# Attention and two quantised convolutions on one core: q's first stacks from two products, three projections later, v's bias in the output projection

## The chip, the cores and the metric

The kernel runs on one core of a Trainium2 chip. The metric is device time in microseconds (us), the median of several executions. A core has five engines with a queue each, worked off in order: TensorE (PE in the profile, with its weight loads as PEld), VectorE (DVE), ScalarE (ACT), GpSimd (POOL) and SyncE (SP). SP, ACT and POOL also issue DMA transfers. Matmuls write to PSUM, a memory of eight banks; a bank holds 512 float32 numbers for each of the 128 partitions.

## What is computed

Input x has four images of 128 channels and 64 x 64 pixels. The first layer is a group norm (8 groups) with self-attention over the 4096 pixels, four heads of 32 channels, and a residual; the second layer is two 3 x 3 convolutions with 3-bit weights, each followed by a batch norm and relu, the second with a residual. The change touches only the first layer:

```python
x_norm = _group_norm(x, norm_w, norm_b)
qkv = jnp.einsum('oc,bchw->bohw', qkv_w, x_norm) + qkv_b[None, :, None, None]
q, k, v = jnp.split(qkv, 3, axis=1)
...
attn = jnp.einsum('bhid,bhjd->bhij', q, k) * scale
attn = jax.nn.softmax(attn, axis=-1)
out = jnp.einsum('bhij,bhjd->bhid', attn, v)
out = out.transpose(0, 1, 3, 2).reshape(b, c, h, w)
out = jnp.einsum('oc,bchw->bohw', proj_w, out) + proj_b[None, :, None, None]
return x + out
```

Since the rows of a softmax sum to one, a constant added to every row of v comes out of the attention unchanged.

## The kernel before

**Norm.** The group norm is folded into the projection weights. `norm_parts` (line 242) returns nine small steps for an image: `zero` to `four` make from the statistics the scaled weights `wn` (128 x 384, the columns of q, k and v) and a column `c`; `five` and `six` multiply `c` with the weights of k and q and make from it and `qkv_b` the two bias columns `b2`; `five_v` and `six_v` make `bvn`, the bias of v spread over 128 partitions. For image 0 the steps run at the start; for the others they are put into an earlier image's blocks.

**Projections.** An image is cut into 8 chunks of 512 pixels. `project_parts` (line 319) gives for a chunk three products (k, q, v), each in three steps: two halves of matmuls (`mm` or `mmv`, four bands of 32 columns each), then the evacuation of the PSUM bank. For k and q (`parts`) ScalarE writes the rounded high part with the bias added, and VectorE the rest, the low part. For v (`evac_v`) VectorE adds `bvn`. High and low parts of k and q go to DRAM (`kd`, `qd`), and are read back stacked by heads: in a tile of k or q two heads lie with their high and low parts in four bands of 32 partitions (`load_k`, four DMAs on SP; `load_q`, eight). Only for chunk 0 of image 0 are they copied straight between tiles, by eight DMAs each (`direct`).

**PSUM.** The pool `pss` has three places of two banks, tag "s", for the scores; at the start the products of k and q use them too. The pool `psa` has two banks, tag "a": one is held by the accumulator `acc` of the running block, the other is used in turn by everything else (products, the small norm matmuls, row sums `l`, the output projection `po`).

**Blocks.** There are 32 blocks, 8 for each image, a block being 512 queries against the image's 4096 keys in 32 steps `kt` of 128 keys. A step is two pairs of heads: `scores(pair)` makes the scores of two heads with four matmuls of 64 x 128 x 512 and has ScalarE take the exponent. `weights(step, half)` multiplies the exponents with v, a half of the queries at a time. The order of all engines' work is written out by hand: three score pairs, three halves of weights, and so on, with scores three pairs ahead:

```python
    run_scores(3)
    while at["half"] < 2 * steps:
        run_scores(3)
        run_weights(3)
```

The row sums are added up by VectorE (`r`, 128 x 2048 a step), and for six steps of a block by DMAs on POOL's queue that accumulate (`rm`, 1 MB each).

**Side work.** `schedule(n, before)` (line 633) lists for block n what is put after which half: `at_half(p, f)`. `ends` are the last halves of the groups of three. `visit(i, first, second, evacuate, split)` puts a product at group end i (with `split` its second half at the next end), and the evacuation one half later, which in the queues is behind the next group's three scores and exponents. For block 0 the products still missing for image 0 are placed at every second group end: k5, v4, k6, v5, k7, q1, v6, v7 at ends 0, 2, 4, 6, 8, 10, 12, 14; `load_k` of a k chunk is put five halves after its end. k chunk j is read first by pair 8j, and v chunk j by half 8j.

**Start.** Lines 588 to 624: the eight x chunks of image 0 are loaded into two tiles, statistics and norm steps follow (with idle matmuls between them), then ten products: k0, q0, k1, v0, k2, v1, k3, v2, k4, v3, with `five_v` and `six_v` after q0, and `load_k` of the next chunk after each v. DMAs of constants are issued on POOL first (lines 115 to 127).

**Later images.** In the third such block of an image (`qn == 2`), `five` is put at end 1, `six` and `five_v` one half later, `six_v` two halves later. A product of k of the next image stands in the same block at end 3. At a block's end `store` (line 546) adds the projection, its bias `bp` and x.

Of the kernel before, what the change touches and what calls it, by code (L numbers as in the profile page):

```python
# [22 lines left out]
P = 128  # L23
# [55 lines left out]
def _fast_body(ctx, tc, x, norm_w, norm_b, qkv_wt, qkv_b, proj_wt, proj_b,  # L79
# [35 lines left out]
    nw, nb = column(norm_w, "nw"), column(norm_b, "nb")  # L115
    wqkv = const.tile([P, 3 * P], F32, name="wqkv")
    nc.gpsimd.dma_start(out=wqkv, in_=qkv_wt)
    bkq = const.tile([P, 2], F32, name="bkq")
    nc.gpsimd.dma_start(out=bkq[:, 0:1], in_=qkv_b[P : 2 * P].rearrange("(c o) -> c o", o=1))
    nc.gpsimd.dma_start(out=bkq[:, 1:2], in_=qkv_b[0:P].rearrange("(c o) -> c o", o=1))  # L120
    bv = const.tile([P, P], F32, name="bv")
    nc.gpsimd.dma_start(out=bv, in_=qkv_b[2 * P : 3 * P].partition_broadcast(P))
    wp = const.tile([P, P], F32, name="wp")
    nc.gpsimd.dma_start(out=wp, in_=proj_wt)
    bp = column(proj_b, "bp")
# [116 lines left out]
    def norm_parts(b, st):  # L242
        mv = small.tile([P, 2], F32, name=f"mv{b}", tag="mv")
        mean = small.tile([P, 1], F32, name=f"mean{b}", tag="mean")
        dv = small.tile([P, 1], F32, name=f"dv{b}", tag="dv")
        gm = {}

        def zero():
            nc.vector.bn_aggr(mv, st.rearrange("p j s -> p (j s)"))


        def one():
            gm[0] = psa.tile([P, FB], F32, name=f"gm{b}", tag="a")
            nc.tensor.matmul(gm[0][:, 0:1], gavg, mv[:, 0:1], start=True, stop=True)

        def two():
            nc.vector.tensor_tensor(dv, mv[:, 0:1], gm[0][:, 0:1], ALU.subtract)
            nc.vector.scalar_tensor_tensor(dv, dv, dv, mv[:, 1:2], ALU.mult, ALU.add)
            nc.vector.tensor_copy(mean, gm[0][:, 0:1])

        def three():
            gm[1] = psa.tile([P, FB], F32, name=f"gv{b}", tag="a")
            nc.tensor.matmul(gm[1][:, 0:1], gavg, dv, start=True, stop=True)

        def four():
# [12 lines left out]
        def five():  # L278
            wn, c, cb = norm[b]
            gm[2] = psa.tile([P, FB], F32, name=f"gb{b}", tag="a")  # L280
            nc.tensor.matmul(gm[2][:, 0:1], wqkv[:, P : 2 * P], c, start=True, stop=True)
            nc.tensor.matmul(gm[2][:, 1:2], wqkv[:, 0:P], c, start=True, stop=True)

        def six():
            b2 = wpool.tile([P, 2], F32, name=f"b2_{b}", tag="b2")
            nc.vector.tensor_tensor(b2, bkq, gm[2][:, 0:2], ALU.subtract)
# [12 lines left out]
        return zero, one, two, three, four, five, six, five_v, six_v  # L299

# [18 lines left out]
    def project_parts(b, j, xin, start=False):  # L319
# [27 lines left out]
        def parts(what, o, dst):  # L347
# [3 lines left out]
            nc.scalar.activation(hi, ps[what], AF.Identity, bias=bias)  # L351
            nc.vector.scalar_tensor_tensor(lo, ps[what], bias, t[:, 0, :], ALU.add, ALU.subtract)  # L352
            if start and j == 0:
                direct(what, t)
            else:
                (nc.sync if start else nc.gpsimd).dma_start(out=dst[b, j].rearrange("s p n -> p s n"), in_=t)  # L356

# [7 lines left out]
        def evac_v():  # L365
            if b == 0:
                v = vs[b, j] = vpool.tile([P, KB, P], F32, name=f"v{b}_{j}", tag="v")
                v = v.rearrange("p i f -> p (i f)")
            else:
                v = staged(1, "v")[:, 0, :]  # L370
            nc.vector.tensor_tensor(v.rearrange("p (i f) -> p i f", f=P),
                                    ps["v"].rearrange("p (i f) -> p i f", f=P),
                                    norm[b][2].unsqueeze(1).to_broadcast([P, KB, P]), ALU.add)
            if b > 0:
                nc.gpsimd.dma_start(out=vd[b, j], in_=v)

# [11 lines left out]
        qs[b, j] = qpool.tile([P, 2, 2, FB], F32R, name=f"q{b}_{j}", tag="q")  # L388
        return qs[b, j]

    def direct(what, t):

        u = k_tile(0, 0) if what == "k" else q_tile(0, 0)
        engines = (nc.sync, nc.gpsimd) if what == "k" else (nc.scalar, nc.sync, nc.gpsimd)
        for g in range(2):
            for c, s in enumerate((0, 2, 1, 3)):
                i, part = divmod(s, 2)
                h = 2 * g + i
                src = t[h * D : (h + 1) * D, :, :]
                eng = engines[(4 * g + c) % len(engines)]  # L400
                if what == "k":
                    eng.dma_start(out=f32(u)[s * D : (s + 1) * D, g, :], in_=src[:, part, :])
                else:
                    eng.dma_start(out=f32(u)[s * D : (s + 1) * D, g, :, :], in_=src)

    def load_k(b, j):
        k = k_tile(b, j)
# [65 lines left out]
    def finish_parts(n):  # L473
# [124 lines left out]
    zero, one, two, three, four, five, six, five_v, six_v = norm_parts(0, st)  # L598
    zero()
    one()  # L600
    keep_warm(3)
# [23 lines left out]

# [7 lines left out]
    def schedule(n, before):  # L633
# [49 lines left out]
        if b + 1 < B:  # L683
# [727 lines left out]
```

## Time and profile before

| what | us |
|---|---|
| median of three runs (2546.02 to 2547.59) | 2547.48 |
| the profiled execution | 2548.74 |
| its span, first to last instruction | 2547.0 |
| first scores of block 0 | 26.66 |
| convolutions, from the last weights on (2231.4) to the end | 315.6 |

| engine | busy in 34.21 to 105.00 us (70.79 us) |
|---|---|
| PE | 70.79 |
| ACT | 62.41 |
| DVE | 61.23 |
| POOL | 7.89 |

The profiled execution's own time is 1.7 us above its span. In the profile a line such as `L456 PE MATMUL acc<-p,v` names the line of the kernel, the engine, the operation, and the tile written and those read. In a timeline the columns are start and duration in us, then the instruction, how many of the same kind follow each other, and in brackets how long the engine had been idle before, and what ended that. A "q" behind an engine (SPq) means its sequencer, which issues DMAs. The ends of matmuls are modelled, so the starts are the better measure.

### The profile page before, as it was taken

To read this page: it belongs to the slowest core of one execution; us is meant where nothing else is said; L and a number is where in the kernel's file an instruction comes from. 1 tells how busy PE (TensorE), PEld (TensorE's weight loads), DVE (VectorE), ACT (ScalarE), POOL (GpSimd) and SP (SyncE) were. 2 spreads that over 40 slices of the span, in tenths; PEclk is the share of its full clock that TensorE was granted. 3 is DMA by queue.
4 is the path that set the end of the run, shared out by engine and by line. 5 is a ranking of instruction groups with operands and counts; after the bars stand their busy time and mean duration, and the time that the engine had idled before them with its cause. 6 is when DMAs were issued, how large, how long until landed. Compare 5 with 4: busy or idle time off the path is not lost.

```text
span 2547.0 us, 65043 instructions
## 1 busy us (share of the span) xinstructions
PE 2509.0 (99%) x28708; PEld 1503.6 (59%) x28708; DVE 2137.2 (84%) x1402; ACT 2087.4 (82%) x2278; POOL 281.6 (11%) x461
## 2 busy tenths in 40 slices
PE   9999999999999999999999999999999999999995
PEld 6555555555555555555555555555555555577774
DVE  6899888889988889889988888889999999954445
ACT  5999888999988999999988899989999999911224
POOL 2111111111011111110111111111000011000000
PEclk9999999999999999999999999999999999999998
DMA  6877667788757667797766666796666666745004
GB/s 193 192 185 169 168 173 181 171 203 182 184 132 190 170 152 169 164 231 164 173 163 172 157 166 158 191 203 150 149 138 144 146 145 149 150 90 160 1 1 166
DMA packets 148954, 403.86 MB, mean 159 GB/s; under 512 B 59416, under 2 KB 60184, under 8 KB 120120
## 3 DMA queue, kind: packets, MB, share of 16 engines
q0 software_dynamic: 45840, 280.39, 48.2%
q1 hardware_dynamic: 100952, 113.60, 16.9%
q10 hardware_dynamic: 1872, 5.64, 0.6%
q8 instruction: 227, 3.72, 0.6%
q14 instruction: 63, 0.52, 0.1%
HBM read 107.48 MB, written 56.42 MB: 64 GB/s over the span
## 4 chain that ended last, share of the span: by engine, by line
PE 92%; issue 3%; DMA 2%; DVE 1%; ACT 1%; ACTq 0%; POOL 0%; SPq 0%; POOLq 0%; DVEq 0%
PE s L442 41%; PE acc L456 36%; PE c L782 9%; DMA rm<-p 2%; PE l L488 1%; PE pq L317 1%; PE pk L317 1%; PE po L317 1%; PE pv L317 1%; DVE r L471 1%; ACT p L444 0%; ACT res L949 0%; DMA xh<-in_x_dram 0%; PE c_last L782 0%; DVE res L948 0%
## 5 line engine op out<-in xcount | busy, mean ns | idle before, releaser
L444 ACT ACTIVATE p<-s 128x1024 f32<-128x1024 f32 x2048 | 1950.5, 1032 | 201.6 <-PE s L442 154.5
L471 DVE TENSOR_TENSOR r<-r,p 128x2048 f32<-128x2048 f32 x768 | 1758.2, 2289 | 65.0 <-ACT p L444 14.5
L442 PE MATMUL s<-q,k 64*128 64x512 f32 x8192 | 1138.6, 409 | 1.7 <-ACT p L444 0.9
L456 PE MATMUL acc<-p,v 128*32 128x256 f32 x16384 | 1026.4, 383 | 0.0
L442 PEld LDWEIGHTS s<-q,k 64*128 64x128 f32 x8192 | 715.4, 184 | 410.3 <-issue 165.3
L456 PEld LDWEIGHTS acc<-p,v 128*32 128x32 f32 x16384 | 462.4, 109 | 483.7 <-issue 248.5
L466 POOL DMA_DIRECT2D rm<-p x160 | 139.5, 872 | 800.4 <-ACT p L444 535.5
L849 ACT COPY cv<-c 128x512 f32<-128x512 f32 x60 | 35.2, 586 | 200.1 <-DVE st L848 200.1
L782 PE MATMUL c<-hi,wq 128*128 128x512 f32 x540 | 139.1, 401 | 1.3 <-issue 1.3
L782 PE MATMUL c<-lo,wq 128*128 128x512 f32 x540 | 138.5, 400 | 0.0
L848 DVE BATCH_NORM_STATS2 st<-c 128x6 f32<-128x512 f32 x60 | 41.9, 699 | 103.9 <-PE c L782 83.4
L782 PEld LDWEIGHTS c<-hi,wq 128*128 128x128 f32 x540 | 101.2, 188 | 30.3 <-issue 2.1
L782 PEld LDWEIGHTS c<-lo,wq 128*128 128x128 f32 x540 | 101.6, 188 | 27.2
L352 DVE SCALAR_TENSOR_TENSOR kst<-pk,b,kst 128x512 fp32r<-128x512 f32 x32 | 24.0, 751 | 83.6 <-PE s L442 68.5
L469 DVE TENSOR_TENSOR r<-p,p 128x2048 f32<-128x2048 f32 x32 | 73.2, 2288 | 12.1 <-ACT p L444 11.1
L352 DVE SCALAR_TENSOR_TENSOR qst<-pq,b,qst 128x512 fp32r<-128x512 f32 x32 | 24.0, 751 | 58.2 <-PE s L442 47.3
L356 POOL DMA_DIRECT2D qd<-qst x31 | 23.6, 760 | 262.7 <-DVE qst L352 220.8
L492 POOL DMA_DIRECT2D r<-rm x31 | 26.2, 844 | 220.4 <-DMA rm<-p 95.1
L356 POOL DMA_DIRECT2D kd<-kst x27 | 20.0, 740 | 175.8 <-DVE kst L352 167.2
L488 PE MATMUL l<-r,ones 128*32 128x256 f32 (+1 forms) x504 | 37.7, 382 | 0.0
L464 POOL DMA_DIRECT2D rm<-p x32 | 17.8, 557 | 176.8 <-ACT p L444 93.4
L351 ACT ACTIVATE kst<-pk,b 128x512 fp32r<-128x512 f32 x32 | 22.3, 699 | 18.2 <-PE pk L317 18.2
(149 smaller groups left out, 739.3 us busy)
## 6 DMA issues: line engine op xcount, KB each, us to landing
rm<-p POOLq DMA_DIRECT2D x192, 1024.0 KB, 7.9
q<-qd SPq DMA_DIRECT2D x248, 128.0 KB
r<-rm POOLq DMA_DIRECT2D x31, 1024.0 KB, 7.6
x<-in_x_dram SPq DMA_DIRECT2D x86, 256.0 KB
k<-kd SPq DMA_DIRECT2D x124, 128.0 KB
qd<-qst POOLq DMA_DIRECT2D x31, 512.0 KB, 5.3
kd<-kst POOLq DMA_DIRECT2D x27, 512.0 KB, 4.8
y<-x POOLq DMA_DIRECT2D x32, 256.0 KB, 6.2
```

Source lines behind the costliest of these rows:

```text
L317: nc.tensor.matmul(out[cs, :], w[:, cs], x, start=True, stop=True)
L352: nc.vector.scalar_tensor_tensor(lo, ps[what], bias, t[:, 0, :], ALU.add, ALU.subtract)
L356: (nc.sync if start else nc.gpsimd).dma_start(out=dst[b, j].rearrange("s p n -> p s n"), in_=t)
L442: nc.tensor.matmul(s[:, i, :], k[r, half, c0 : c0 + P], q[r, half, part, :], start=(part == 0), stop=(part == 1))
L444: nc.scalar.activation(pts[step][:, 2 * half : 2 * half + 2, :], s, AF.Exp, scale=SCALE)
L456: nc.tensor.matmul(acc[n][h * D : (h + 1) * D, cs], v[:, kt % KB, h * D : (h + 1) * D], pt[:, h, cs], start=(kt == 0 and half == 0), stop= ...
L466: nc.gpsimd.dma_start(out=msum[n], in_=pt, accum_op=ALU.add)
L469: nc.vector.tensor_tensor(rsum[n], pts[step - 1], pt, ALU.add)
L471: nc.vector.tensor_tensor(rsum[n], rsum[n], pt, ALU.add)
L488: nc.tensor.matmul(t["l"][h * D : (h + 1) * D, cs], ones, r[:, h, cs], start=first, stop=end)
L782: nc.tensor.matmul(ps.rearrange("p (r w) -> p r w", w=W), w[:, tap, :], part[:, r0 + kh : r0 + kh + RB, kw : kw + W], start=(n == 0), stop ...
L848: nc.vector.bn_stats(st[:, b * NB + c, :], ps[:, j, :])
```

## The change

It has four parts. (1) The first q tile of image 0 is no longer made from a product that is copied by eight DMAs. `direct_q` makes two products, one for each pair of heads, whose four bands of output partitions already lie as the stack needs them (each head twice); ScalarE writes the high part, VectorE the low part, straight into the tile. It needs the bias of q in the same stacked order, two columns more in `b2` for image 0. (2) Three products (k4, v2, v3) go from the start into block 0, whose side work is spread anew. (3) The bias of v is taken out of v and added by the output projection: `five` makes a third column, `seven_v` multiplies it with the projection's weights, and `eight_v` adds `proj_b`. (4) v's bank is copied by ScalarE, without a bias.

```diff
-    bkq = const.tile([P, 2], F32, name="bkq")
-    nc.gpsimd.dma_start(out=bkq[:, 0:1], in_=qkv_b[P : 2 * P].rearrange("(c o) -> c o", o=1))
-    nc.gpsimd.dma_start(out=bkq[:, 1:2], in_=qkv_b[0:P].rearrange("(c o) -> c o", o=1))
-    bv = const.tile([P, P], F32, name="bv")
-    nc.gpsimd.dma_start(out=bv, in_=qkv_b[2 * P : 3 * P].partition_broadcast(P))
+    bkqv = const.tile([P, 5], F32, name="bkqv")
+    for c, o in enumerate((P, 0, 2 * P)):
+        nc.gpsimd.dma_start(out=bkqv[:, c : c + 1],
+                            in_=qkv_b[o : o + P].rearrange("(c o) -> c o", o=1))
+    for band in range(4):
+        nc.gpsimd.dma_start(
+            out=bkqv[band * D : (band + 1) * D, 3:5],
+            in_=qkv_b[0:P].rearrange("(g i d) -> i d g", i=2, d=D)[band // 2])
...
-            cb = wpool.tile([P, P], F32, name=f"cb{b}", tag="cb")
-            nc.vector.tensor_copy(cb, c.to_broadcast([P, P]))
-            norm[b] = [wn, c, cb]
+            norm[b] = [wn, c, None]
...
-            nc.tensor.matmul(gm[2][:, 0:1], wqkv[:, P : 2 * P], c, start=True, stop=True)
-            nc.tensor.matmul(gm[2][:, 1:2], wqkv[:, 0:P], c, start=True, stop=True)
+            for u, o in enumerate((P, 0, 2 * P)):
+                nc.tensor.matmul(gm[2][:, u : u + 1], wqkv[:, o : o + P], c, start=True, stop=True)
+            if b == 0:
+                for g in range(2):
+                    for band in range(4):
+                        h = 2 * g + band // 2
+                        nc.tensor.matmul(gm[2][band * D : (band + 1) * D, 3 + g : 4 + g],
+                                         wqkv[:, h * D : (h + 1) * D], c, start=True, stop=True)
...
-        def five_v():
-            gm[3] = psa.tile([P, FB], F32, name=f"gw{b}", tag="a")
-            nc.tensor.matmul(gm[3][:, 0:P], norm[b][2], wqkv[:, 2 * P : 3 * P],
-                             start=True, stop=True)
-
-        def six_v():
-            bvn = wpool.tile([P, P], F32, name=f"bvn{b}", tag="bvn")
-            nc.vector.tensor_tensor(bvn, bv, gm[3][:, 0:P], ALU.subtract)
-            norm[b][2] = bvn
+        def seven_v():
+            gm[3] = psa.tile([P, FB], F32, name=f"gp{b}", tag="a")
+            nc.tensor.matmul(gm[3][:, 0:1], wp, norm[b][1][:, 2:3], start=True, stop=True)
+
+        def eight_v():
+            norm[b][2] = small.tile([P, 1], F32, name=f"bpn{b}", tag="bpn")
+            nc.vector.tensor_tensor(norm[b][2], bp, gm[3][:, 0:1], ALU.add)
...
-            nc.vector.tensor_tensor(v.rearrange("p (i f) -> p i f", f=P),
-                                    ps["v"].rearrange("p (i f) -> p i f", f=P),
-                                    norm[b][2].unsqueeze(1).to_broadcast([P, KB, P]), ALU.add)
+            nc.scalar.copy(v, ps["v"])
...
+    def direct_q(xin):
+
+        u = q_tile(0, 0)
         for g in range(2):
...
+            ps = pss.tile([P, 2, FB], F32, name=f"pq_first{g}", tag="s")[:, 0, :]
+            for band in range(4):
+                h = 2 * g + band // 2
+                nc.tensor.matmul(ps[band * D : (band + 1) * D, :], norm[0][0][:, h * D : (h + 1) * D],
+                                 xin, start=True, stop=True)
+            bias = norm[0][1][:, 3 + g : 4 + g]
+            nc.scalar.activation(u[:, g, 0, :], ps, AF.Identity, bias=bias)
+            nc.vector.scalar_tensor_tensor(u[:, g, 1, :], ps, bias, f32(u)[:, g, 0, :],
+                                           ALU.add, ALU.subtract)
...
-            nc.vector.scalar_tensor_tensor(t["x"], t["o"], bp, t["x"], ALU.add, ALU.add)
+            nc.vector.scalar_tensor_tensor(t["x"], t["o"], norm[b][2], t["x"], ALU.add, ALU.add)
...
-    for what, j in (("k", 0), ("q", 0), ("k", 1), ("v", 0), ("k", 2), ("v", 1), ("k", 3), ("v", 2),
-                    ("k", 4), ("v", 3)):
+    for what, j in (("k", 0), ("q", 0), ("k", 1), ("v", 0), ("k", 2), ("v", 1), ("k", 3)):
+        if what == "q":
+            direct_q(halves[0][:, 0, :])
+            continue
         for f in first_chunk(j, what, True):
             f()
-        if what == "q":
-            five_v()
-            six_v()
         if what == "v":
             load_k(0, j + 1)
+    load_k(0, 3)
+    seven_v()
+    eight_v()
...
-            for i, what, j in ((0, "k", 5), (2, "v", 4), (4, "k", 6), (6, "v", 5), (8, "k", 7),
-                               (10, "q", 1), (12, "v", 6), (14, "v", 7)):
+            for i, what, j in ((0, "k", 4), (2, "v", 2), (3, "v", 3), (4, "q", 1), (6, "k", 5),
+                               (8, "v", 4), (9, "v", 5), (10, "k", 6), (12, "v", 6), (13, "k", 7),
+                               (15, "v", 7)):
...
-                at_half(ends[1] + 1, late[b][7])
-                at_half(ends[1] + 2, late[b][8])
+                at_half(ends[3], late[b][7])
+                at_half(ends[3] + 1, late[b][8])
```

The copy of chunk 0 of k by eight DMAs stays, as `direct_k`.

More of the change, by code (lines that the diff above doesn't have):

```diff
@@ L272, in four @@
             nc.vector.tensor_scalar(wn, wqkv, a, None, ALU.mult)
-            cb = wpool.tile([P, P], F32, name=f"cb{b}", tag="cb")
-            nc.vector.tensor_copy(cb, c.to_broadcast([P, P]))
-            norm[b] = [wn, c, cb]
+            norm[b] = [wn, c, None]
         def five():
-            wn, c, cb = norm[b]
+            wn, c, _ = norm[b]
             gm[2] = psa.tile([P, FB], F32, name=f"gb{b}", tag="a")
-            nc.tensor.matmul(gm[2][:, 0:1], wqkv[:, P : 2 * P], c, start=True, stop=True)
@@ L284, in six @@
         def six():
-            b2 = wpool.tile([P, 2], F32, name=f"b2_{b}", tag="b2")
-            nc.vector.tensor_tensor(b2, bkq, gm[2][:, 0:2], ALU.subtract)
+            n = 3 if b else 5
+            b2 = wpool.tile([P, 5], F32, name=f"b2_{b}", tag="b2")
+            nc.vector.tensor_tensor(b2[:, :n], bkqv[:, :n], gm[2][:, :n], ALU.subtract)
             norm[b][1] = b2
-        def five_v():
-            gm[3] = psa.tile([P, FB], F32, name=f"gw{b}", tag="a")
-            nc.tensor.matmul(gm[3][:, 0:P], norm[b][2], wqkv[:, 2 * P : 3 * P],
-                             start=True, stop=True)
@@ L294, in six_v @@
-        def six_v():
-            bvn = wpool.tile([P, P], F32, name=f"bvn{b}", tag="bvn")
-            nc.vector.tensor_tensor(bvn, bv, gm[3][:, 0:P], ALU.subtract)
-            norm[b][2] = bvn
-        return zero, one, two, three, four, five, six, five_v, six_v
+        def seven_v():
[4 more added lines that the diff above has]
+            nc.vector.tensor_tensor(norm[b][2], bp, gm[3][:, 0:1], ALU.add)
@@ L303, in _fast_body @@
+        return zero, one, two, three, four, five, six, seven_v, eight_v
     kd, qd, vd = {}, {}, {}
@@ L353, in parts @@
             if start and j == 0:
-                direct(what, t)
+                direct_k(t)
             else:
@@ L389, in q_tile, with direct_k @@
         return qs[b, j]
-    def direct(what, t):
-        u = k_tile(0, 0) if what == "k" else q_tile(0, 0)
-        engines = (nc.sync, nc.gpsimd) if what == "k" else (nc.scalar, nc.sync, nc.gpsimd)
-        for g in range(2):
[L396 to L404, printed above, removed]
+    def direct_k(t):
+        u = k_tile(0, 0)
+        for c, (g, s) in enumerate((g, s) for g in range(2) for s in (0, 2, 1, 3)):
+            i, part = divmod(s, 2)
+            h = 2 * g + i
+            (nc.sync, nc.gpsimd)[c % 2].dma_start(out=f32(u)[s * D : (s + 1) * D, g, :],
+                                                  in_=t[h * D : (h + 1) * D, part, :])
+    def direct_q(xin):
+        u = q_tile(0, 0)
+        for g in range(2):
+            ps = pss.tile([P, 2, FB], F32, name=f"pq_first{g}", tag="s")[:, 0, :]
[7 more added lines that the diff above has]
+                                           ALU.add, ALU.subtract)
     def load_k(b, j):
@@ L597, in _fast_body @@
         nc.vector.bn_stats(st[:, j, :], halves[j // 4][:, j % 4, :])
-    zero, one, two, three, four, five, six, five_v, six_v = norm_parts(0, st)
+    zero, one, two, three, four, five, six, seven_v, eight_v = norm_parts(0, st)
     zero()
```

## The prediction

> **What bounds the kernel now.** I read the page's busy shares first, then the sum of waits, then the timeline of the first 80 us.
>
> ```profile
> span 2547.0 us, 65043 instructions
> ## 1 busy us (share of the span) xinstructions
> PE 2509.0 (99%) x28708; PEld 1503.6 (59%) x28708; DVE 2137.2 (84%) x1402; ACT 2087.4 (82%) x2278; POOL 281.6 (11%) x461
> ```
>
> PE (TensorE) is the bound: only 38 us of the span are without a matmul. An edit therefore pays by what it takes from PE's work or waits, not by what DVE or ACT save. The timeline shows the start:
>
> ```profile
> 16.22 1.07 PE L317 MATMUL pk<-xh,wn 128*32 128x256 f32 x16
> ...
> 19.72 2.01 ACTq L404 DMA_DIRECT2D q<-qst  x3
> ...
> 23.91 1.08 PE L317 MATMUL pv<-wn,xh 128*32 128x128 f32 x32 [0.87 <-DVE v L371]
> ...
> 26.66 0.74 PE L442 MATMUL s<-q,k 64*128 64x512 f32 x4
> ...
> 28.09 2.06 PE L442 MATMUL s<-q,k 64*128 64x512 f32 x12 [0.69 <-DVE v L371]
> ...
> 34.21 1.23 PEld L442 LDWEIGHTS s<-q,k 64*128 64x128 f32 x12 [0.41 <-issue]
> ...
> 34.98 2.85 ACT L444 ACTIVATE p<-s 128x1024 f32<-128x1024 f32 x3 [1.04 <-PE s L442]
> ...
> 37.24 1.23 PEld L442 LDWEIGHTS s<-q,k 64*128 64x128 f32 x12 [0.41 <-ACT p L444]
> ...
> 37.71 0.70 ACT L351 ACTIVATE kst<-pk,b 128x512 fp32r<-128x512 f32 x1
> ...
> 39.94 1.00 PEld L317 LDWEIGHTS pv<-wn,xh 128*32 128x32 f32 x32
> ```
>
> Read: ten products fill PE from 16.22 to 26.66. From 34.21 on PE runs groups of three score pairs and three weight halves: 3.03 us without a product (34.21 to 37.24), 3.90 with one (the next starts at 41.14), so a product costs 0.87 us. ACT's exps lag: those of the group that starts at 34.21 run from 34.98 to 37.83, and only then comes the evacuation (37.71) of the product that PE made at 33.23.
>
> POOL's part of the same timeline:
>
> ```profile
> 67.52 0.74 POOL L356 DMA_DIRECT2D kd<-kst  x1 [12.51 <-DVE kst L352]
> 68.25 0.91 POOL L466 DMA_DIRECT2D rm<-p  x1
> ```
>
> That is the tile k7 whose product began at 60.70: its write is issued 6.8 us later, its load (SP, the last four of the sixteen issues of L411) at 71.62 to 75.25. In the trace's packet records SP's queue moves that load only from 76.0 to 79.4, when the rm transfer issued at 68.25 has ended. Product to loaded tile: 18.7 us. k6 gives the same: 46.87 to 65.6. Today both have plenty of time.
>
> **What the Trainium skill says.** "PSUM — Partial Sum Buffer", section "PSUM bank collisions raise a hardware error": two engines must not touch one bank and quadrant at once, and a kernel guards this with semaphores. So a product waits for the evacuation of its bank; the wait at 23.91 (0.87 us on DVE) is one. "DMA: Bandwidth & Descriptors", "Issuing engines are not separate DMA queues": all queues share the 16 engines and interleave. The sharing agrees; fair turns as in its "Queues, rings and completion order" don't show, since SP's queue got next to nothing for 4 us. "TensorEngine Tiling (Array Packing)", "Key Properties": different column tiles work in parallel; the 16 instructions of a product start over 0.87 us, though each is shown as 0.38, which agrees.
>
> **The change part by part.** Sums are against the profiled execution: 2548.74 us, span 2547.0; its median of three is 2547.48, so 1.3 lower.
>
> *Start.* `five` gets one matmul of one column (a gb matmul takes 0.22 from start to start: 15.68, 15.90) and eight of 32 columns. No row shows 32 columns into one; the product's weight loads follow each other at 37 ns (16 in 0.59), so 16 of them are 0.6 (bounds 0.3 and 1.0). k0's product moves from 16.2 to 17.0. q now costs two products, +0.87. Gone are gw with its gap, from 17.97 to 18.50, 0.5; three products, 2.6; ACT's three q DMAs, behind which k1's evacuation waited to 21.78. PE then runs eight products from 17.0, 7.0 us: 24.0, and `seven_v` to 24.4. The pss banks come free in time (k0's low part by 19.65, where k1 needs it at 19.6; q's by 20.5 and 21.3). k0's copies are issued from 18.9 to 21.5 and land by 23.1 to 24.0 (the POOL ones took 2.1 to 3.1). First scores at 24.4 instead of 26.66. The wait at 28.09 (1.1 us with its PEld gap) goes: its sequencer also waited for DMA semaphores up to 27.98, which I take for q's last copies. After the six-pair ramp, which ACT's exps set, the next group starts at 30.9 instead of 34.21: **-3.3** (bounds -1.5 and -4.5).
>
> POOL's queue: four more DMA issues of 0.56. By the eight landings before, which already held gamma back to 9.40, its last issue ends at about 14.5; the power for rsqrt starts at 14.62. Nothing, or up to 0.5 late. k1's write (SP, about 22.3, 3.2 to 4.75 to land) and load (3 us) end by 30, needed at 32: hidden.
>
> *Three products into the first block*: they were on PE's path and stay on it: 3 x 0.87 = **+2.6**. The rest of their cost is waits.
>
> *Neighbouring group ends.* Before, products stand at every second end. Now v2-v3-q1, v4-v5-k6 and v6-k7 stand at neighbouring ones: five times. psa has two banks and acc holds one, so the second product waits for the first one's copy, now on ACT, whose queue has that group's three exps ahead. Group start S: exps end at S+3.62, the copy starts at S+3.5 (as kst at 37.71) and takes 0.59 (L849's row, same shape): S+4.1. PE wants the bank at S+2.70 (39.94 less 37.24). 1.44 each, **+7.2** (bounds 4.5 and 9). All score groups wait behind that product.
>
> *k6 and k7 later.* k6 moves from end 4 to 10, k7 from 8 to 13. Group starts after 30.9, adding 3.03, 3.90 with a product, 5.34 with one that waits: 33.9, 37.8 (v2), 43.2 (v3), 48.5 (q1), 51.5, 55.4 (k5), 58.5, 62.4 (v4), 67.7 (v5), 73.1 (k6), 76.1, 80.0 (v6), 85.3 (k7), 88.4, 92.3 (v7), 95.3. A product's weight loads begin 1.2 before the start it stands at. k6's, at 71.9, has its tile needed by pair 48, first of the group at 88.4: 16.5 us later. It has landed 18.7 after: +2.2. k7 has 14.5 us from 84.1 to pair 56, third of the group at 95.3, with that shift. Its load comes after block 1's q load (1 MB, 5 to 6 us at the before run's rate) on SP and meets the next rm transfer: in between 15 and 19 us; I take +3.0. Together **+5.2** (bounds 0 and 10). Scores wait on it and all else behind. k4's write goes from SP to POOL, 0.74 ahead of the first rm; by the same 18.7 it has landed before 50 and is needed at 63: hidden, as k5 is (21.8 us from product to need).
>
> *Later images, three times.* five's extra matmul 3 x 0.22 = 0.66. gw goes: its groups took 3.59, 4.31 and 3.58 against 3.03, so -2.4. `seven_v` now sits at end 3, where k's product also wants a psa bank: k waits for `eight_v` on DVE. Matmul, semaphore, 0.15 add: 0.65 twice, and 1.4 where DVE has a 2.29 us r add ahead (block 10). Sum **+1.0** (bounds -1 and +4). v's bias out of 32 copies saves 0.68 us each on DVE, off the path; ACT's 0.59 fit, as kst's 0.70 do today, into 0.17 us a group plus 0.87 a product. Nothing; if that cover is gone, 24 x 0.3.
>
> Sum: -3.3 + 2.6 + 7.2 + 5.2 + 1.0 = **+12.7**: 2561.4 in a profiled execution, 2560 as a median.
>
> **Rivals.**
> A, the forecast: 2560, 2556 to 2566.
> B, the waits for banks come, but k6 and k7 land in time, since PE's own waits give their transfers time: +7.5, 2555. For it: my k figures hang on whether an rm transfer stands before them. Against: both k tiles measured took 18.7.
> C, k7's load falls behind a second rm transfer: another 8 us (rm's median landing is 7.9): 2568.
> D, not slower: the banks come free early, because ACT has caught up while PE waits, so a copy costs PE at most 0.9 us at each of the five places and k lands in time. Then -3.3 + 2.6 + 1.0 + at most 4.5: 2548 to 2552. It decides at 0.95 a place: five of them are then 4.8, and the sum is 5.1 us, 0.2%. For it: ACT is idle 0.8 us before the next exps. Against: the copy is queued behind exps which can't start before the group's own scores, wherever ACT stood.
> That the start doesn't gain (k0's own copies land after 24.4) makes each case about 1 to 2 us worse.
>
> **How the numbers follow.** A 0.50, B 0.21, C 0.11, D 0.18. The likeliest gives 2560. The range takes in B and most of A's and C's bounds: 2551 to 2568. A measurement of this kernel tells about 0.2% (5 us) from no change; A, B and C lie beyond it: slower 0.82. D splits into 0.15 within and 0.03 faster, which would take a start at its best bound and DVE's relief removing the three later stalls (0.8, 0.9 and 2.0 us at 604, 1151 and 1690).
>
> **What would show it.** Right: first scores at about 24.4 with no DMA on ACT's queue before; PE waiting for ACT's v copies five times by 1.0 to 1.5 in the first block; group starts there 5.3 apart at those places; a gap of PE before kt 24 or 28 released by a DMA of k. Wrong: copies of v before the exps of their group, PE going on in 3.9 us groups, or a first score after 26. If block 0 ends less than 5 us later than now, the forecast fails; if the extra time lies after block 1, the cause is one I haven't named.

## The result, and the profile after

| kernel | median, us | range | executions |
|---|---|---|---|
| before | 2547.53 | 2546.02 to 2549.99 | 6 |
| changed | 2565.06 | 2562.47 to 2565.84 | 6 |

The ratio is 1.0068, with a 95% interval of 1.0055 to 1.0081. The changed kernel is 17.5 us slower. Its profiled execution took 2564.58 us, and its span is 15.7 us longer than that of before. The page's first part, in the changed kernel:

```profile
span 2562.7 us, 65043 instructions
## 1 busy us (share of the span) xinstructions
PE 2515.3 (98%) x28732; PEld 1506.1 (59%) x28732; DVE 2120.0 (83%) x1367; ACT 2100.9 (82%) x2311; POOL 283.1 (11%) x464
```

PE (TensorE) was without a matmul for 38.0 us before and is now for 47.4 us: 9.4 of the 15.7. The other 6.3 are busy time, though PE has only 24 more matmuls. So part of the loss is PE working more slowly, which a sum of waits can't show. The timeline shows where it happens. In the changed kernel the scores are L456 and their exps L458, the weights L470, the products L325, v's copy L379, a kd write L364, a k load L425, a q load L436, an rm transfer L480. The start and the first neighbouring group ends:

```profile
23.41 1.20 PE L456 MATMUL s<-q,k 64*128 64x512 f32 x8
...
30.06 1.24 PEld L456 LDWEIGHTS s<-q,k 64*128 64x128 f32 x12 [0.41 <-issue]
...
37.00 1.23 PEld L456 LDWEIGHTS s<-q,k 64*128 64x128 f32 x12 [0.20 <-issue]
...
37.78 2.85 ACT L458 ACTIVATE p<-s 128x1024 f32<-128x1024 f32 x3 [0.77 <-PE s L456]
...
40.50 0.61 ACT L379 COPY v<-pv 128x512 f32<-128x512 f32 x1
41.16 1.08 PE L325 MATMUL pv<-wn,xh 128*32 128x128 f32 x32 [1.06 <-ACT v L379]
42.17 1.23 PEld L456 LDWEIGHTS s<-q,k 64*128 64x128 f32 x12 [0.20 <-issue]
```

Read it as the prediction read the old one. The second group starts at 30.06 instead of 34.21. The group at 37.00 takes 5.17 us to the next start, where one with a product took 3.90, because its v product waits for the copy of the v before it. That copy stands behind three exps.

The end of block 0, in the same timeline:

```profile
82.56 1.07 PE L325 MATMUL pk<-xh,wn 128*32 128x256 f32 x16 [1.07 <-ACT v L379]
...
84.44 4.75 SPq L436 DMA_DIRECT2D q<-qd  x8
...
87.81 0.46 PE L456 MATMUL s<-q,k 64*128 64x512 f32 x1 [1.16 <-DMA k<-kd]
...
88.83 0.74 POOL L364 DMA_DIRECT2D kd<-kst  x1 [10.43 <-DVE kst L360]
...
89.01 2.90 PE L456 MATMUL s<-q,k 64*128 64x512 f32 x11 [0.73 <-DMA k<-kd]
...
92.48 0.87 POOL L480 DMA_DIRECT2D rm<-p  x1 [2.91 <-ACT p L458]
...
94.47 5.03 SPq L425 DMA_DIRECT2D k<-kd  x4
...
102.81 0.76 PE L456 MATMUL s<-q,k 64*128 64x512 f32 x1 [4.22 <-DMA k<-kd]
...
104.14 1.19 PE L456 MATMUL s<-q,k 64*128 64x512 f32 x3 [0.56 <-DMA k<-kd]
105.25 2.79 PE L470 MATMUL acc<-p,v 128*32 128x256 f32 x24
107.97 2.33 PE L456 MATMUL s<-q,k 64*128 64x512 f32 x12
```

The waits at 87.81 and at 89.01 are for k6, those at 102.81 and 104.14 for k7, whose product is the one at 82.56: its tile arrives 20.2 to 21.6 us later. The three halves of weights at 105.25 take 2.79 us where the same 24 matmuls take 1.50 elsewhere. In the trace's record of the granted clock PE is at half speed from 88.97 to 92.38 and from 102.62 to 109.45 us, one and two steps of 3.41 us, and from 7.05 us on at full speed in the rest of the attention. The windows view, from its second row on cut at these steps (the columns are the window, its length, busy time and instructions of PE, PEld, DVE, ACT and POOL, then PEclk, DMA share and GB/s):

```profile
78.40:83.56 5.16, 4.09 (x57) 2.14 (x53) 4.85 (x3) 3.36 (x5) 0.01 (x1) 1.00 1.09 249
85.56:88.97 3.41, 1.56 (x24) 0.57 (x13) 1.18 (x2) 2.19 (x3) 0.14 (x1) 1.00 1.09 247
88.97:92.38 3.41, 3.37 (x19) 2.25 (x23) 3.38 (x2) 2.15 (x3) 0.60 (x1) 0.50 1.07 224
92.38:102.62 10.24, 6.21 (x100) 3.72 (x92) 9.18 (x5) 5.89 (x7) 0.87 (x1) 1.00 0.98 219
102.62:109.45 6.83, 6.08 (x36) 2.96 (x38) 0.68 (x1) 1.24 (x2) 0.00 (x0) 0.50 0.22 81
109.45:112.86 3.41, 3.41 (x42) 2.06 (x40) 0.74 (x1) 3.07 (x4) 0.85 (x1) 1.00 0.38 79
```

The first row is a group with a bank wait of 1.07 us, at full clock. In the second PE is idle for 1.85 of 3.41 us, in its waits for k6, and the next step is at half speed. The fourth ends with the wait for k7, and two steps at half speed follow. PE's 3.37 and 6.08 us of work at half speed would have taken about half as long at full clock, so the slow clock cost about 4.7 us.

Block 1's first scores, which follow the last pair of block 0 in the group that starts at 114.69 (before: 97.84), come at 115.26 instead of 98.41, 16.85 us later. From there to the end the offset stays between 15.7 and 18.6. So the whole loss is made in block 0. By starts of groups:

| part | us |
|---|---|
| second group start, 34.21 to 30.06 | -4.15 |
| three products moved into the block, 0.87 each | +2.6 |
| five groups of 5.17 for 3.90 | +6.3 |
| k6: groups of 4.25 and 6.57 for 3.03 and 3.90 (waits 1.9) | +3.9 |
| k7: groups of 10.57 and 3.69 for 3.03 each (waits 4.8) | +8.2 |
| sum to block 1 | +16.85 |
| later images: gb +0.7, gw -2.4, gp and pk +2.8 | +1.1 |
| other stalls of later blocks that differ | -2.2 |

The last two rows take the sum to 15.75.

### The profile page after: what moved, and what is told of

Read it like the earlier page. It is cut to its first block, busy times and chain, and to the rows that moved or that the text cites. A ratio compares the mean times of both kernels' runs of the same rounds, so it can differ in the third digit from the quotient of the medians.

```text
span 2562.7 us, 65043 instructions
## 1 busy us (share of the span) xinstructions
PE 2515.3 (98%) x28732; PEld 1506.1 (59%) x28732; DVE 2120.0 (83%) x1367; ACT 2100.9 (82%) x2311; POOL 283.1 (11%) x464
## 4 chain that ended last, share of the span: by engine, by line
PE 90%; issue 5%; DMA 2%; POOL 1%; DVE 1%; ACT 1%; SPq 0%; ACTq 0%; POOLq 0%; DVEq 0%
PE s L456 40%; PE acc L470 36%; PE c L799 9%; DMA rm<-p 2%; PE l L502 1%; PE po L325 1%; PE pq L325 1%; PE pk L325 1%; PE pv L325 1%; ACT res L966 0%; DVE r L485 0%; PE c_last L799 0%; DMA wqkv<-in_L_conv_qkv_w_dram 0%; DMA k<-kd 0%; DMA kd<-kst 0%
## 5 line engine op out<-in xcount | busy, mean ns | idle before, releaser
L458 ACT ACTIVATE p<-s 128x1024 f32<-128x1024 f32 x2048 | 1951.5, 1034 | 208.3 <-PE s L456 167.2
L456 PE MATMUL s<-q,k 64*128 64x512 f32 x8192 | 1141.3, 410 | 8.8 <-DMA k<-kd 6.7
L470 PE MATMUL acc<-p,v 128*32 128x256 f32 x16384 | 1027.4, 383 | 0.0
L456 PEld LDWEIGHTS s<-q,k 64*128 64x128 f32 x8192 | 716.8, 185 | 417.8 <-issue 173.1
L470 PEld LDWEIGHTS acc<-p,v 128*32 128x32 f32 x16384 | 463.1, 109 | 485.2 <-issue 250.9
L480 POOL DMA_DIRECT2D rm<-p x160 | 139.2, 870 | 789.2 <-ACT p L458 580.7
L364 POOL DMA_DIRECT2D qd<-qst x31 | 23.0, 741 | 292.4 <-DVE qst L360 238.2
L364 POOL DMA_DIRECT2D kd<-kst x28 | 20.7, 740 | 193.7 <-DVE kst L360 181.8
L562 POOL DMA_DIRECT2D y<-x x32 | 21.4, 670 | 128.9 <-DVE x L561 128.7
```

What stands on the lines that cost most here:

```text
L456: nc.tensor.matmul(s[:, i, :], k[r, half, c0 : c0 + P], q[r, half, part, :], start=(part == 0), stop=(part == 1))
L458: nc.scalar.activation(pts[step][:, 2 * half : 2 * half + 2, :], s, AF.Exp, scale=SCALE)
L470: nc.tensor.matmul(acc[n][h * D : (h + 1) * D, cs], v[:, kt % KB, h * D : (h + 1) * D], pt[:, h, cs], start=(kt == 0 and half == 0), stop= ...
L480: nc.gpsimd.dma_start(out=msum[n], in_=pt, accum_op=ALU.add)
```

## The experiments

The theory was the table above: three products moved into the block bring bank waits, late tiles and a slow clock, and the other parts of the change gain a little. The rivals were that the other parts cost time too (v's copy on ScalarE, the bias by the projection), that the bank is late for another reason than the order of the queue, and that k is late by its own path and not by the rm transfers. Executions of before on the same chips had medians of 2547.47 to 2547.92. Runs 2 to 6 and 10 are one execution each: they are read by their profiles, and their times only where several us matter.

**1. The products put back**, all else of the change kept:

```diff
-    for what, j in (("k", 0), ("q", 0), ("k", 1), ("v", 0), ("k", 2), ("v", 1), ("k", 3)):
+    for what, j in (("k", 0), ("q", 0), ("k", 1), ("v", 0), ("k", 2), ("v", 1), ("k", 3), ("v", 2),
+                    ("k", 4), ("v", 3)):
...
-    load_k(0, 3)
...
-            for i, what, j in ((0, "k", 4), (2, "v", 2), (3, "v", 3), (4, "q", 1), (6, "k", 5),
-                               (8, "v", 4), (9, "v", 5), (10, "k", 6), (12, "v", 6), (13, "k", 7),
-                               (15, "v", 7)):
+            for i, what, j in ((0, "k", 5), (2, "v", 4), (4, "k", 6), (6, "v", 5), (8, "k", 7),
+                               (10, "q", 1), (12, "v", 6), (14, "v", 7)):
```

> The changed kernel with part 2 undone alone: k4, v2 and v3 are products of the start again, and block 0 has the eight products at every second group end as before. Theory (the loss is all in block 0: five waits for v's bank, 6.3 us, and the late tiles k6 and k7, 12.1 us with what follows them): no wait of PE in block 0, groups of 3.03 and 3.90 us, first scores about 26.0, block 1's first scores within 2 us of the kernel before's 98.4; about 2546 us, 0.1% or less below the kernel before. Rival 1 (v's copy on ScalarE or v's bias in the projection costs time in all blocks): 2550 us or more, with the loss spread over the blocks. Rival 2 (q's two products in place of eight DMAs cost more than they give): first scores after 27, about 2550.

Measured: 2545.49 us (13 executions), ratio 0.9993 (0.9984 to 1.0001). Block 0 has no PE wait after its ramp, its groups take 3.03 and 3.90, and block 1 starts 2.0 us sooner than before. Of these 2.0, 1.2 come from the input's statistics, which end at 11.26 us in this execution and at 12.50 in before's; that isn't shown to be the edit's. All of the loss is in the moved products and what hangs on them.

**2. The moves alone**: before, with the change's two lists and its `load_k(0, 3)`.

```diff
-    for what, j in (("k", 0), ("q", 0), ("k", 1), ("v", 0), ("k", 2), ("v", 1), ("k", 3), ("v", 2),
-                    ("k", 4), ("v", 3)):
+    for what, j in (("k", 0), ("q", 0), ("k", 1), ("v", 0), ("k", 2), ("v", 1), ("k", 3)):
...
+    load_k(0, 3)
...
-            for i, what, j in ((0, "k", 5), (2, "v", 4), (4, "k", 6), (6, "v", 5), (8, "k", 7),
-                               (10, "q", 1), (12, "v", 6), (14, "v", 7)):
+            for i, what, j in ((0, "k", 4), (2, "v", 2), (3, "v", 3), (4, "q", 1), (6, "k", 5),
+                               (8, "v", 4), (9, "v", 5), (10, "k", 6), (12, "v", 6), (13, "k", 7),
+                               (15, "v", 7)):
```

> The kernel before with part 2 alone: three products moved into block 0, q by copies, v's bias added by VectorE as it leaves PSUM. Theory: the moves alone bring the loss. The start hardly gains, since q's copies land at 27.98 as before (first scores 25.5 to 26.7, the second pair near 28); in block 0 PE waits at the same five places for the bank, now by VectorE, whose adds of 2.29 us stand before the copy: 0.4 to 1.5 us each; k6 and k7 late by much the same 10 to 12 us with the slow clock after them. Block 1's first scores 15 to 22 us later than before, 2563 to 2569 us in all. Rival (the waits come from ScalarE's copies or from q's new path): block 1 no more than 5 us later, about 2552.

Measured: 2569.0 us, block 1 20.4 us later than before, and an offset of 20.2 to 21.1 from there to the end. Scores start at 24.96 and wait 3.3 us in three places for q's copies, which the change's direct q doesn't have. The five places now depend on v's evacuation by DVE and are uneven, with groups of 4.24, 3.87, 7.34, 4.77 and 4.26; at the second PE doesn't wait, and the fourth is long only because it runs at the slow clock after the third. The third in the timeline:

```profile
60.69 7.00 DVE L471 TENSOR_TENSOR r<-r,p 128x2048 f32<-128x2048 f32 x3
...
67.61 0.68 DVE L371 TENSOR_TENSOR v<-pv,bvn 128x512 f32<-128x512 f32 x1
...
68.34 1.77 PE L317 MATMUL pv<-wn,xh 128*32 128x128 f32 x32 [2.55 <-DVE v L371]
...
70.04 2.54 PE L442 MATMUL s<-q,k 64*128 64x512 f32 x12
```

v's evacuation stands behind three row-sum adds, and after the wait of 2.55 us the product and the scores take 1.77 and 2.54 where 1.06 and 1.66 are usual. So it doesn't take ScalarE to bring bank waits; VectorE with work ahead of the evacuation brings them too. k6 and k7 are late here too (groups of 5.93 and 7.9, 8.74 and 3.65).

**3. k5 to k7 earlier**, q1 later; neighbouring ends stay (v2, v3, k5; v4, v5, k6; v6, q1), so there are still five products that want the bank of the one before:

```diff
-            for i, what, j in ((0, "k", 4), (2, "v", 2), (3, "v", 3), (4, "q", 1), (6, "k", 5),
-                               (8, "v", 4), (9, "v", 5), (10, "k", 6), (12, "v", 6), (13, "k", 7),
+            for i, what, j in ((0, "k", 4), (2, "v", 2), (3, "v", 3), (4, "k", 5), (6, "v", 4),
+                               (7, "v", 5), (8, "k", 6), (10, "k", 7), (12, "v", 6), (13, "q", 1),
```

> The changed kernel with another order of the same eleven products in block 0: k5, k6 and k7 at group ends 4, 8 and 10 (6, 10 and 13 in the change), still with five products right behind a v. Theory (the late tiles are due to the distance between product and first reading): the waits for k6 and k7 go with the slow clock after them, 12.1 us, the five waits of 1.27 us for the bank stay; block 1 starts 4 to 6 us later than in the kernel before, about 2552.5 us. Rival (SP's queue or the DMA engines can't keep up with eleven products): PE still waits for a k tile by 3 us or more, 2557 or more.

Measured: 2553.99 us. There is no wait for k and no slow clock left; five groups of 5.15 to 5.18 are, and block 1 is 4.6 us later than before, where the table without its k rows gives -4.15 + 2.6 + 6.3 = 4.8. The timeline at the second set of neighbouring ends:

```profile
58.29 1.08 PE L325 MATMUL pv<-wn,xh 128*32 128x128 f32 x32 [1.06 <-ACT v L379]
...
63.46 1.07 PE L325 MATMUL pk<-xh,wn 128*32 128x256 f32 x16 [1.06 <-ACT v L379]
```

**4. v's copy ahead of the exps**: the product and its copy at the same group end, in the change's order.

```diff
-                visit(i, *first_chunk(j, what, False), split=False)
+                if what == "v":
+                    for f in first_chunk(j, what, False):
+                        at_half(ends[i], f)
+                else:
+                    visit(i, *first_chunk(j, what, False), split=False)
```

> The changed kernel with one thing moved: in block 0 ScalarE's copy of v is issued right behind its product, ahead of the next group's three exps, not one weight half later. Theory (the wait of 1.27 us at five places is ScalarE's queue order: exps stand before the copy): all five waits go, those groups take 3.90 instead of 5.17 us; the exps are not late, since ScalarE is free then. k6 has 1.3 us less, so the waits for k6 and k7 stay or grow by 1 to 2 us. 2559 to 2561 us. Rival (the wait is the bank's or the copy's own time, wherever it stands): groups of 4.6 us or more there, and no more than 3 us gained.

Measured: 2558.08 us. All five bank waits are gone; the groups take 3.88 to 3.91. The timeline where the first one was:

```profile
36.88 1.67 PE L456 MATMUL s<-q,k 64*128 64x512 f32 x12
37.02 0.59 ACT L379 COPY v<-pv 128x512 f32<-128x512 f32 x1
37.66 2.86 ACT L458 ACTIVATE p<-s 128x1024 f32<-128x1024 f32 x3
...
39.80 1.06 PE L325 MATMUL pv<-wn,xh 128*32 128x128 f32 x32
40.78 1.66 PE L456 MATMUL s<-q,k 64*128 64x512 f32 x12
```

The copy runs in ACT's idle time before the exps, at 37.02 instead of 40.50, and the next v doesn't wait. Block 1 is 12.0 us late instead of 16.8. That is 4.8 of the 6.3: PE now comes sooner to the pairs that need k6 and k7, and waits longer for them (12.0 + 4.15 - 2.6 = 13.5, against 12.1); k5's tile is now late too, by 0.50 us.

**5. Two rm transfers taken out** of block 0, those of steps 19 and 24, whose row sums VectorE adds instead:

```diff
-        if kt in MOVED:
+        if kt in MOVED and not (n == 0 and kt in (19, 24)):
```

> The changed kernel with one thing taken from beside the late loads: in block 0 the sums of steps 19 and 24 are added by VectorE and not by the accumulating DMA rm of 1 MB (the result is the same). Theory (an rm transfer in flight holds back SP's loads of k6 and k7, as the packet records show): both tiles land 3 to 6 us sooner after their product, and the waits with the slow clock after them fall from 12.1 us to between 2 and 7 us; about 2555 to 2560 us. Rival (the chain of evacuation, write and load is too long by itself, whatever else moves): the waits stay above 9 us, 2562 or more; DVE's two more adds of 2.29 us add nothing to PE's path in either case.

Measured: 2557.4 us. The wait for k6 is gone. The timeline at k7:

```profile
93.81 1.19 PE L456 MATMUL s<-q,k 64*128 64x512 f32 x8
93.95 1.71 SPq L425 DMA_DIRECT2D k<-kd  x4
...
97.05 0.47 PE L456 MATMUL s<-q,k 64*128 64x512 f32 x1 [2.05 <-DMA k<-kd]
...
98.10 0.70 PE L456 MATMUL s<-q,k 64*128 64x512 f32 x3 [0.58 <-DMA k<-kd]
98.73 2.55 PE L470 MATMUL acc<-p,v 128*32 128x256 f32 x24
```

The four issues of the load take 1.71 us instead of 5.03, the wait is 2.6 us instead of 4.8, and k6 and k7 cost 4.9 us instead of 12.1. The rm transfers make more than half of what k's lateness costs; the rest is the place of k7 in the order, since it still comes too late without them. The last row also shows that waits of 2.05 and 0.58 us are enough to slow PE (2.55 for the weights): of the step from 95.62 to 99.03 PE was idle for 2.01 us, and the step after it is at half speed.

**6. Idle matmuls before k7 is needed**, 18 of 128 x 128 x 128 (36 instructions in the profile), to see whether the slow stretch after the wait is the clock:

```diff
+        if n == 0:
+            at_half(ends[16], lambda: keep_warm(18))
```

> The changed kernel with 18 idle matmuls of 128x128x128 (about 4 us) put where PE waits for k7, ahead of the group of pairs 54 to 56. They compute nothing that is used. Theory (after a wait of 4 us PE runs at half of its clock for some us, which makes up about 3.4 us of the 8.2 us lost around k7): the tile lands at the same time, but PE then runs at full clock, and block 0 ends 2 to 3.5 us sooner than in the changed kernel. Rival (the slow stretch comes from the DMAs or from SBUF traffic): the same clock of 0.5 after the wait, and no gain, or a loss of up to 1 us.

Measured: 2560.73 us, block 1 13.1 us late instead of 16.8. The timeline and, below it, the windows view of the step with the waits for k6 and of the stretch after the wait for k7:

```profile
97.24 4.29 PE L318 MATMUL idle<-gavg 128*128 128x128 f32 x36 [1.07 <-ACT v L379]
101.46 2.04 PE L456 MATMUL s<-q,k 64*128 64x512 f32 x12
103.42 1.50 PE L470 MATMUL acc<-p,v 128*32 128x256 f32 x24
```

```profile
87.57:90.98 3.41, 2.23 (x16) 1.49 (x20) 3.05 (x3) 1.32 (x3) 0.74 (x1) 1.00 1.07 224
...
102.00:107.00 5.00, 5.00 (x58) 2.77 (x58) 2.29 (x1) 4.23 (x5) 0.05 (x1) 1.00 0.38 134
```

The clock stays at 1.00, and the weights after the wait take 1.50 us instead of 2.79. k7's two groups lose 5.7 us instead of 8.2. k7's tile may have come up to 1.5 us sooner in this run, so the gain of 2.5 us at k7 is an upper value for the clock alone.

k6's groups lost 2.5 instead of 3.9, and that is not the edit's. k6 was waited for as in the change (1.22 and 0.77 us), but here a boundary of the 3.41 us steps, at 87.57, fell into the first wait. Neither step held more than 1.18 us of idle time, and the clock stayed at 1.00 (first row). At full clock 2.0 us of waiting cost 2.5.

**7. Products back, and `seven_v` one group end earlier**, so that it no longer takes the bank at the end where k's product wants it:

```diff
-                at_half(ends[3], late[b][7])
-                at_half(ends[3] + 1, late[b][8])
+                at_half(ends[2], late[b][7])
+                at_half(ends[2] + 1, late[b][8])
```

The reason is in the changed kernel's timeline in block 10:

```profile
756.49 0.38 PE L301 MATMUL gp<-b,wp 128*128 128x1 f32 x2
...
757.50 0.15 DVE L305 TENSOR_TENSOR bpn<-bp,gp 128x1 f32<-128x1 f32 x1
757.70 1.07 PE L325 MATMUL pk<-x,wn 128*32 128x256 f32 x16 [0.83 <-DVE bpn L305]
```

> Part 2 undone (as in the first run of this study) and seven_v and eight_v put one group end earlier for the images 1 to 3, so that k's product at end 3 finds its bank free. Theory (the wait for eight_v is 0.25, 0.83 and 0.25 us of idle PE and with the bank's turnaround some 0.3 to 1 us each): 1 to 2 us below that run, about 2544 us, 0.1 to 0.2% below the kernel before. Rival (the wait only moves to the next place): no difference to that run.

Measured: 2543.75 us (21 executions), ratio 0.9986 (0.9980 to 0.9993). The waits of pk after gp are gone. This is the fastest version of the study, 3.7 us below before on the same chip.

**8. The change kept, its waits mended**: runs 3, 4 and 7's edits together on the changed kernel. Theory: the loss goes; rival: the moves then gain by themselves and beat run 7.

```diff
+            for i, what, j in ((0, "k", 4), (2, "v", 2), (3, "v", 3), (4, "k", 5), (6, "v", 4),
+                               (7, "v", 5), (8, "k", 6), (10, "k", 7), (12, "v", 6), (13, "q", 1),
...
+                if what == "v":
+                    for f in first_chunk(j, what, False):
+                        at_half(ends[i], f)
...
+                at_half(ends[2], late[b][7])
```

> All of the change kept, with three repairs: k5 to k7 early as in the third run, v's copy right behind its product as in the fourth, seven_v one group end earlier. Theory: none of the waits in block 0 is left, and the three moved products cost what they cost at the start, so that the time is that of the run with the products back and seven_v earlier, 2543.5 to 2547 us. Rival (moving products off the start gains by itself, as first scores come 2.4 us earlier): 2 us or more below that run.

Measured: 2546.76 us (13 executions), ratio 0.9996 (0.9988 to 1.0005). First scores come at 22.98, and the waits for banks and for k are gone, but block 1 starts only 2.0 us sooner than before, as in run 1. The rival falls: the products' time comes back in the block in full. One small wait is new, in block 0's last group:

```profile
95.80 2.35 PE L456 MATMUL s<-q,k 64*128 64x512 f32 x12
...
96.71 0.30 PEld L456 LDWEIGHTS s<-q,k 64*128 64x128 f32 x4 [0.38 <-DMA q<-qd]
```

Block 1's first scores wait for q1's tile, whose product run 3's order moved to end 13, and the group takes 3.71 us instead of 3.03. By block 2 this kernel is 1.35 us ahead of before, and run 7's 1.83. That is most of the 0.7 us between the spans of the two profiled executions; the medians differ by 3.0, and the rest of that is open.

**9. q by copies in run 7's kernel**, to size part 1 alone:

```diff
-                direct_k(t)
+                direct(what, t)
...
-        if what == "q":
-            direct_q(halves[0][:, 0, :])
-            continue
```

> The run with the products back and seven_v earlier, but the first q tile again made of one product and eight copies by DMA: what is left are v's bias in the projection, v's copy on ScalarE and seven_v earlier. Theory (q's direct way costs one product more, 0.87 us, and saves the second score pair's wait for the copies and k1's late evacuation, so that it gives about 1 us at the start and nothing later): block 1's first scores 0.5 to 1.5 us later than in that run (there 1.8 us before the kernel before's); about 2545 us. Rival (the direct way costs as much as it saves): no difference, within 0.3 us at block 1.

Measured: 2546.55 us (13 executions), ratio 0.9997 (0.9989 to 1.0005). Block 1 starts 0.9 us sooner than before, with direct q (run 7) 1.8. The statistics end at 11.63 and 11.61 in these two executions, so the 0.9 between them is direct q's. They end at 12.50 in before's, which makes up the 0.9 that is left without it. The timeline shows what direct q takes away:

```profile
19.22 1.96 ACTq L410 DMA_DIRECT2D q<-qst  x3
...
26.44 1.03 PE L448 MATMUL s<-q,k 64*128 64x512 f32 x4 [0.45 <-DMA q<-qst]
...
27.62 1.63 PE L448 MATMUL s<-q,k 64*128 64x512 f32 x11 [0.16 <-DMA q<-qst]
```

Here PE's waits are put down to q's copies; in the kernel before, the one at 28.09 was put down to DVE's v. The prediction took it for q's last copies, and this run supports that.

**10. v copied by VectorE** in run 1's kernel. Run 1 loses no time in block 23, where before has a stall, and the theory was that ScalarE's copies bring this gain of about 2 us:

```diff
-            nc.scalar.copy(v, ps["v"])
+            nc.vector.tensor_copy(v, ps["v"])
```

> The run with the products back alone, with v copied from PSUM by VectorE and not by ScalarE (still without a bias). Theory (the 2 us that all kernels with ScalarE's copies gain within block 23, where the kernel before had PE waiting for VectorE's weighing at 1694.7, come from the copies that left VectorE): block 24's first scores lie no longer 2 us further ahead of block 23's offset, and the time is about 2 us above that run's. Rival (that gain is due to something else, such as when DMAs meet): it stays, and the time is the same within 0.5 us in the profile.

Measured: 2544.6 us; the offset to before still goes from -1.3 at block 23 to -3.3 at block 24. The theory falls. Run 2, which keeps v's bias add on VectorE, doesn't have the gain (+20.6 and +20.4 there), so it may be the missing bias; that wasn't tried, and the cause stays open.

## Why the prediction was right or wrong

The forecast of slower, its place (block 0) and its three mechanisms held, and the median of 2565 lies within A's 2556 to 2566. The sum was too small: 12.7 us were forecast, and 15.7 (spans of the profiled executions) or 17.5 (medians) came. That it came so near owes something to luck, since stalls of later blocks, put at nothing, gave 2.2 us back.

- *Start*, -3.3: measured -4.15, within the bounds. `five`'s eight small matmuls were costed at 0.6 us and took 0.14 (from 15.84 to k0's product at 15.98), and the scores came at 23.41, not 24.4. The input's statistics end at 12.50 before, at 11.87 after, and at 11.1 to 12.2 in the experiments, so 0.6 of the 4.15 is not shown to be the change's; the rest is close to the forecast.
- *Three products*, +2.6: held; run 8 shows that moving them gains nothing by itself.
- *Neighbouring group ends*, +7.2: 6.3. The copy started 3.5 us after the group, and took 0.61, as forecast. The wait was counted from the product's weight loads, which without a wait begin 0.2 us ahead of its matmuls (35.80 and 36.01); after a wait both begin together (41.16), so it cost 1.27 a place instead of 1.44. Rival D decided at 0.95 a place and had ACT catching up; run 4 shows that the copy's place in ACT's queue does it.
- *k6 and k7 later*, "Together **+5.2** (bounds 0 and 10)": this is the step that failed, with 12.1. Its mechanism was right, and for k6 its figure too (18.5 us from product to the end of the last wait, where 18.7 was taken). Two terms were mis-sized. For k7 the prediction said "in between 15 and 19 us; I take +3.0", which is 17.5 us, less than the 18.7 that it had read for both tiles. It was 20.2 to 21.6: SP's queue moved the load from 99.5 to 105 us only, after the rm transfer issued at 92.48 had moved its data, and its write to DRAM, issued at 88.83, let it be issued only at 94.47. The waits alone came to 1.9 for k6 and 4.8 for k7, 6.7 in all. Of the other 5.4, about 4.7 are a term that the sum lacked: after such a wait PE runs at half clock for 3.41 us or a multiple. Run 5 shows the first by removing rm transfers, and run 6 the second by keeping the clock at k7.
- Rival C put k7 behind a second rm transfer, 8 us more. k7 did stand behind one, though not by a full transfer, and the measured median lies between A's 2560 and C's 2568.
- *Later images*, +1.0: +1.1, with gb +0.22, gw gone and gp and pk +2.8. *Later stalls* were put at nothing; the two at 604 and 1690 went, one of about 1.5 us near 1170 came, -2.2 in all.
- *POOL's queue* was costed at nothing: its last constant's issue ended at 13.98 and the power started at 14.00, so it was hidden, with no slack.

## What to carry to other kernels

A product that is moved into a block whose bound is PE costs what it cost before, and its evacuation has to be placed too: where a bank is shared, put the copy ahead of the work that waits for the block's own results. A moved producer needs its whole path counted up to the loaded tile, with the large transfers that it will meet, and a wait on PE costs more than itself where it lowers the clock for the work after it (k7: 8.2 for 4.8; k6: 3.9 for 1.9 in the change, but 2.5 for 2.0 in run 6, where the clock held). Where moving a step gains nothing in the ideal case (run 8), leave it, and take the rest of the change (run 7).

## What the runs showed of the hardware

- The clock drops after shorter waits than expected. The Trainium skill, "TensorE: Matmul & The Clock Gate", sections "What's actually happening" and "HAM oscillation — how this bites in real kernels", gives half speed after an idle window of about 3.4 us, and the rule to avoid idle gaps longer than that. The half speed and the length agree: 0.50 after 4.22 us, in steps of 3.41 us. But the idle time need not fill a step. In all twelve traces, with the attention divided into these steps from the first full speed on, a step at full speed in which PE was idle for 1.70 us or more (nine, in the change and in runs 2, 4 and 5) is followed by half speed, and none with 1.63 or less is. A step at half speed is followed by full speed if PE was busy throughout (idle for at most 0.04 us, nine steps), and by half speed again if it was idle for 0.51 or more (five). So here about half a step without matmuls was enough, in one wait or in several, and a wait of 2 us that two steps shared cost no speed (run 6). The measurement decides.
- Here an accumulating 1 MB rm transfer on POOL's queue left SP's queue next to nothing. The Trainium skill, "DMA: Bandwidth & Descriptors", section "Queues, rings and completion order", has the queues take turns; that doesn't show. In the packet records of the changed kernel k6's tile and the q load moved on SP's queue only from 85 to 92 us, when the rm transfer issued at 77.49 was ending (it landed at 86.96). Run 5, without it, had no wait for k6.
